# A transformer stack on one core: one product of the second feed-forward by 12-bit parts, and other engines for the last rows

## The chip, the cores and the metric

The kernel runs on one core of a Trainium2 chip. The time is device time in microseconds (us); a difference is judged between runs of the two kernels on the same chip. The core's engines are TensorE (PE, with its weight loads PEld), VectorE (DVE), ScalarE (ACT), GpSimd (POOL) and SyncE (SP), which here issues transfers. All times below are microseconds. L284 means line 284 of the kernel.

## The reference

Eight blocks are added one after the other to x, which has 2 x 256 tokens of 256 numbers, all in fp32: four times a cross-attention and a feed-forward, each behind a layer norm and a gate.

```python
x = x + tanh(g_xattn[0]) * _L0_xattn_ref(_layernorm(x), ctx_2048)
x = x + tanh(g_ffn[0])   * _L0_ffn_ref(_layernorm(x), ...)
x = x + tanh(g_xattn[1]) * _L1_xattn_ref(_layernorm(x), ctx_2048, ...)
x = x + tanh(g_ffn[1])   * _L1_ffn_ref(_layernorm(x), w_gate_up, w_down)
...
x = x + tanh(g_ffn[3])   * _L3_ffn_ref(_layernorm(x), ...)
```

Two of them are touched. The second feed-forward, with 1024 hidden columns:

```python
gate_up = jnp.einsum('bsh,oh->bso', h_shard, w_gate_up)
gate, up = jnp.split(gate_up, 2, axis=-1)
h = jax.nn.silu(gate) * up
out = jnp.einsum('bsi,hi->bsh', h, w_down)
```

And the last one, a mixture of 8 experts with the two best for each token (`_moe_routed`) beside a shared MLP of 704 hidden columns: each token gets the rows that its two experts made, times their weights, and the shared result. What matters of it is the end, `y.at[tok].add(w * gathered)`, `routed + shared`, and the gated addition to x.

## The kernel before

The 512 tokens are four tiles of 128 (n = 0 to 3); x stays in SBUF as four tiles of 128x256. The whole program is one function, `flamingo`. A scheduler places the instructions on each engine, except where the text fixes the order: `inline` (L222) chains an instruction behind the one before it in the list `line` (VectorE and what else is given to it), `pool_line` (GpSimd) or `pe_line` (TensorE).

**Two ways of multiplying in fp32.** A whole product (`chain`, L282) of 128x512 is two fp32 matmuls. A product by parts first cuts each operand into its top 12 bits and the rest, as fp32r: `weight_parts` (L625) cuts on VectorE (L596), copies the top on ScalarE (L631), subtracts on GpSimd (L632) to get the rest, and forms the difference of top and scaled rest on VectorE (L633). This last instruction can be held back and issued later (`held`). `three` (L640) then issues four matmuls of one sum ("same", L644) and two of another ("cross", L646), in two PSUM tiles, and `joined` (L648) joins them: ScalarE scales the cross sum out of PSUM (L649), VectorE adds the same sum (L650).

**The second feed-forward** (from L1108) runs over 8 chunks of 128 hidden columns. `whole1` makes a whole product, `parts1` one by parts, `silu1` is ScalarE's silu, `gated1` VectorE's product into hT (L1137). Chunks 0 to 2 are whole; of chunk 3 the gate is by parts and the up product whole; chunks 4 to 7 are by parts, with the PSUM pools taken in turn (ps_mm with 4 buffers, ps_acc with 2, ps_tr with 2). The parts of the gate's columns (gate_parts) are made earlier, beside the attention; the parts of the up columns of chunks 4 and 5, then 6 and 7 (up_parts) are made here by `columns_parts`, in two pieces of 128x512. Then `down` multiplies hT with the down weights for each of the four token tiles. On SP follow the loads for the next block, and on GpSimd the zeroing of the arrays that later take scattered rows (L1202 to L1205).

**The end.** The experts' rows lie in DRAM (yg). For each token tile n, L2029 loads its two rows (k = 0 and 1) into rows[n], tiles 0 and 2 on SP's queue, 1 and 3 on ScalarE's. The shared MLP's sum of a tile is made by `shared_down` on TensorE; `add_to_x` (L286) adds scaled rows or sums to x on VectorE (L287). `final(n)` (L2033) adds a tile's two rows: for tile 2, row 1 goes over ScalarE (scaling, L2037) and GpSimd (addition, L2038). Tile 3's two rows are added by TensorE instead, as two more matmuls of its sum, with diagonal matrices that hold the weights (`spread`, made by GpSimd, L1916). `store(n)` (L2042) writes a tile on SP's queue.

The lines of chunks 2 and 3, and the order of the end:

```python
    gated1(2, silu1(pa), pb)
    diffs.pop()()
    g = parts1(3, gate_parts, 3, ps_tr, "tr")
    pb = mm()
    whole1(3, up1, pb)
    columns_parts(up_parts, ffn1[1], 4, 6, 2, diffs)
    gated1(3, silu1(g), pb)
    diffs.pop()()
```

Of the kernel before, what the change touches and what calls it, by code (L numbers as in the profile page):

```python
# [17 lines left out]
F32 = mybir.dt.float32  # L18
F32R = mybir.dt.float32r
I32 = mybir.dt.int32  # L20
U8 = mybir.dt.uint8
AF = mybir.ActivationFunctionType
ALU = mybir.AluOpType
AX = mybir.AxisListType

P = 128
NT = 4
D = 256
# [22 lines left out]
def flamingo(ctx: ExitStack, tc: tile.TileContext, a: dict, out: bass.AP):  # L51
    nc = tc.nc

    def pool(name, bufs, space=None):
        kw = {} if space is None else {"space": space}
        return ctx.enter_context(tc.tile_pool(name=name, bufs=bufs, **kw))

    const = pool("const", 1)
    q4 = pool("q4", Q4)
    q2 = pool("q2", Q2)  # L60
    q1 = pool("q1", 4)
# [4 lines left out]
    x = const.tile([P, NT, D], F32, name="x")  # L66
# [73 lines left out]
    ident = const.tile([P, P], F32, name="ident")  # L140
# [49 lines left out]
    def gf(layer):  # L190
        return tg[:, 4 + layer : 5 + layer]
# [30 lines left out]
    def inline(i, line=line):  # L222
        if line:
            if line[-1] is not None:
                behind(i, line[-1], "in the order of the text")
            line[:] = [i]
        return i
# [35 lines left out]
    def batch(t, k, ts=slice(0, T)):  # L263
        return t[:, ts.start // 256 : ts.stop // 256, k, :]
# [14 lines left out]
    def mm(shape=None):  # L279
        return ps_mm.tile(shape or [P, 512], F32, tag="mm", name="mm")  # L280

    def chain(dst, pairs):  # L282
        for i, (lhsT, rhs) in enumerate(pairs):
            inline(nc.tensor.matmul(dst, lhsT=lhsT, rhs=rhs, start=(i == 0), stop=(i == len(pairs) - 1)), pe_line)  # L284

    def add_to_x(n, acc, scalar, cols=slice(0, D)):  # L286
        return inline(nc.vector.scalar_tensor_tensor(x[:, n, cols], acc, scalar, x[:, n, cols], ALU.mult, ALU.add))  # L287
# [231 lines left out]
    for s in range(18):  # L519
        n = s // 4  # L520
# [53 lines left out]
    ps_mm = pool("ps_mm", 4, bass.MemoryType.PSUM)  # L574
# [51 lines left out]
    def weight_parts(dst, src, t, last=None, held=None):  # L626

        i = inline(cut(t, src))
        if last is not None:
            behind(i, last, "in turn, where there is room")  # L630
        nc.scalar.copy(dst[0], t)  # L631
        nc.gpsimd.tensor_sub(dst[1], src, t)  # L632
        diff = lambda: inline(nc.vector.scalar_tensor_tensor(dst[2], dst[1].bitcast(F32), -1.0 / EPS, t, ALU.mult, ALU.add))  # L633
        if held is None:
            diff()
        else:
            held.append(diff)
        return i

    def three(same, cross, left, right):  # L640

        for k in range(2):
            for i in range(2):
                inline(nc.tensor.matmul(same, lhsT=left(i, k), rhs=right(i, k), start=(k == 0 and i == 0), stop=(k == 1 and i == 1)), pe_line)  # L644
        for k in range(2):
            inline(nc.tensor.matmul(cross, lhsT=left(2, k), rhs=right(2, k), start=(k == 0), stop=(k == 1)), pe_line)  # L646

    def joined(dst, same, cross, scale=1.0):  # L648
        nc.scalar.mul(dst, cross, -EPS * scale)  # L649
        return inline(nc.vector.scalar_tensor_tensor(dst, same, (1.0 + EPS) * scale, dst, ALU.mult, ALU.add))  # L650
# [197 lines left out]
    def l1_scales(sums, part):  # L848

        r, g = (small.tile(list(sums.shape), F32, tag=f"{nm}{sums.shape[2]}", name=nm, bufs=2) for nm in ("rsum", "gsum"))  # L850
        inline(nc.vector.reciprocal(r, sums))
        inline(nc.vector.tensor_scalar_mul(g, r, gx(1)))
        for t, v in ((all_t, sums), (all_r, r)):
            nc.gpsimd.tensor_add(t[:, 0:part], t[:, 0:part], v.rearrange("p i j -> p (i j)"))
        return g

    def l1_turned(d, groups=4):
        tr = ps_acc.tile([P, 2, P], F32, tag="acc", name="tr1")
        rows = 32 * groups
        for i in range(2):  # L860
            inline(nc.tensor.transpose(tr[:, i, 0:rows], d[0:rows, i * P : (i + 1) * P], ident[0:rows, 0:rows]), pe_line)
        sums = small.tile([P, 2, groups], F32, tag=f"sum{groups}", name="sum1", bufs=2)
        nc.scalar.copy(sums, tr[:, :, 0:rows:32])
        return l1_scales(sums, 2 * groups)
# [15 lines left out]
    ffn1 = []  # L880
# [45 lines left out]
    def columns_parts(w, src, base, c, chunks, held=None):  # L926

        t = q2.tile([P, 2, chunks * P], F32, tag="q2", name="c_top")
        cols = slice((c - base) * P, (c - base + chunks) * P)
        weight_parts([w[:, j, :, cols] for j in range(3)],  # L930
                     src.rearrange("p (k e) -> p k e", k=2)[:, :, c * P : (c + chunks) * P], t, held=held)
# [10 lines left out]
    for h in range(16):  # L942
        g, hl = h // 4, h % 4
# [8 lines left out]
        for b in range(B):  # L952
# [12 lines left out]
            if h and h % 2 == 0:  # L965
                if b == 0:
                    sums1 = l1_sums([totals.pop((h - 2 + i, c)) for i in range(2) for c in range(B)])
                else:
                    scale = l1_turned(sums1)
# [23 lines left out]
            if hl and g < 3:  # L993
                n = 2 * (hl - 1) + b
# [9 lines left out]
    scale = l1_turned(sums1, 3)  # L1004
# [4 lines left out]
    t = totals.pop((15, 1))  # L1009
# [15 lines left out]
    scale = l1_scales(sums, 2)  # L1025
# [25 lines left out]
    def negatives(z):  # L1051
        t = q2.tile(list(z.shape), F32, tag="q2", name="fm")
        inline(nc.vector.tensor_scalar_min(t, z, 0.0))
        nc.scalar.activation(t, t, AF.Exp)
        return t
# [60 lines left out]
    gate1, up1 = (w.rearrange("p (k e) -> p k e", k=2) for w in ffn1[0:2])  # L1116
# [3 lines left out]
    def whole1(c, w, p, ts=slice(0, T)):  # L1120
        chain(p[:, ts], [(w[:, k, c * P : (c + 1) * P], batch(xT, k, ts)) for k in range(2)])

    def parts1(c, w, base, pool, tag):
        same, cross = (pool.tile([P, T], F32, tag=tag, name="gu1") for _ in range(2))
        cols = slice((c - base) * P, (c - base + 1) * P)
        three(same, cross, lambda i, k: w[:, i, k, cols], lambda i, k: batch(x_parts[i], k))
        t = q2.tile([P, T], F32, tag="q2", name="gu1")
        joined(t, same, cross)
        return t

    def silu1(src):
        s = q2.tile([P, T], F32, tag="q2", name="silu")
        silus[:] = [nc.scalar.activation(s, src, AF.Silu)]
        return s

    def gated1(c, s, up):
        inline(nc.vector.tensor_mul(hT[c // 2][:, c % 2, :], s, up))  # L1137
# [12 lines left out]
    for c in range(2):  # L1150
        for w, p in zip((gate1, up1), ps[c]):
            whole1(c, w, p, lasts)
        s = silu1(ps[c][0])
# [3 lines left out]
    pa, pb = mm(), mm()  # L1157
    whole1(2, gate1, pa)
    whole1(2, up1, pb)
    diffs = []  # L1160
    columns_parts(up_parts, ffn1[1], 4, 4, 2, diffs)
    gated1(2, silu1(pa), pb)
    diffs.pop()()
    g = parts1(3, gate_parts, 3, ps_tr, "tr")
    pb = mm()
    whole1(3, up1, pb)
    columns_parts(up_parts, ffn1[1], 4, 6, 2, diffs)
    gated1(3, silu1(g), pb)
    diffs.pop()()
    pools = deque([(ps_mm, "mm"), (ps_acc, "acc"), (ps_tr, "tr")])  # L1170
    for c in range(4, 8):
        g, u = [], []
        for w, base, to in ((gate_parts, 3, g), (up_parts, 4, u)):
            to.append(parts1(c, w, base, *pools[0]))
            pools.rotate(-1)
            if to is g:
                s = silu1(g[0])
# [130 lines left out]
    t = negatives(early)  # L1308
# [193 lines left out]
    t, u = rtile(), place  # L1502
# [45 lines left out]
    t = rtile()  # L1548
# [13 lines left out]
    row = q2.tile([P, T], F32, tag="q2", name="row")  # L1562
# [241 lines left out]
    es, t = l3_exps(0, ps3[0])  # L1804
    g = l3_sums(0, t)
    es1, t1 = l3_exps(1, ps3[1])
    load_table(AF.Silu, exps[-1], "the feed-forward's table")
    for b in range(B):
        if b:
            es, g = es1, l3_sums(1, t1)  # L1810
# [101 lines left out]
    kept = const.tile([P, 2, NT], F32, name="kept")  # L1912
    nc.vector.tensor_scalar(w[:, 0, :], w[:, 1, :], -0.5, 0.5, ALU.mult, ALU.add)
    nc.vector.tensor_scalar(w[:, 1, :], w[:, 1, :], 0.5, 0.5, ALU.mult, ALU.add)
    nc.vector.scalar_tensor_tensor(kept, slot3, float(E * CAP), w, ALU.is_lt, ALU.mult)
    spread = q1.tile([P, 2, P], F32, tag="q1", name="spread")  # L1916
    for k in range(2):
        nc.gpsimd.tensor_scalar(spread[:, k, :], ident, kept[:, k, 3:4], None, ALU.mult)
    nc.vector.tensor_scalar_mul(kept, kept, gf(3))

    def shared_down(n, more=[]):
        acc = ps_acc.tile([P, D], F32, tag="acc", name="acc")
        chain(acc, [(hS[c // 2][:, c % 2, n * P : (n + 1) * P], shd[:, c, :]) for c in range(6)] + more)
        return acc
# [5 lines left out]
    for g in range(5):  # L1930
        t = q4.tile([P, 2, D + 1], F32, tag="q4", name="xg_sb")
# [93 lines left out]
    accs = [shared_down(n) for n in range(2)]  # L2025
    rows = []
# [3 lines left out]
        after_all(read, returned)  # L2030
        rows.append(o)

    def final(n):  # L2033
        for k in (1, 0):
            if (n, k) == (2, 1):
                t = q1.tile([P, D], F32, tag="q1", name="row2")
                nc.scalar.activation(t, rows[n][:, k, :], AF.Copy, scale=kept[:, k, n : n + 1])  # L2037
                nc.gpsimd.tensor_add(x[:, n, :], x[:, n, :], t)  # L2038
                continue
            add_to_x(n, rows[n][:, k, :], kept[:, k, n : n + 1])  # L2040

    def store(n):  # L2042
        nc.sync.dma_start(out[n * P : (n + 1) * P, :], x[:, n, :])

    for n in range(2):
        add_to_x(n, accs[n], gf(3))
    accs = [shared_down(2), shared_down(3, [(spread[:, k, :], rows[3][:, k, :]) for k in range(2)])]
    add_to_x(2, accs[0], gf(3))
    final(0)
    store(0)  # L2050
    for n in (1, 2):
        final(n)
        store(n)
    add_to_x(3, accs[1], gf(3))
    store(3)
    line.clear()
# [656 lines left out]
```

## Time and profile before

| what | us |
|---|---|
| median of 3 runs (545.74 to 546.36) | 546.23 |
| the profiled execution, whole | 545.36 |
| its span | 543.5 |
| TensorE busy | 535.0 |
| VectorE busy | 332.3 |
| ScalarE busy | 238.1 |
| GpSimd busy | 124.7 |

The span is that of one execution under the profiler, on the one core, from the first instruction to the end of the last; the mean granted TensorE clock in it was 0.998 of full speed. What the execution took beyond the span (1.86) lies before and after it. TensorE's busy time hides what it does: the page's groups separate whole products (L284) and those by parts (L644, L646).

The page's rows of the 40 slices, each of 13.6 us, show where TensorE is not full: the first and the last slice, and no other.

```
PE   8999999999999999999999999999999999999996
PEclk9999999999999999999999999999999999999999
DMA  8910120000004000040000404599030799614013
```

The second feed-forward lies in the slices from about 340 to 380, the end of the kernel in the last one. In a row of the profile's timeline, the first number is the start in the span, the second the duration, then engine, line, operation, the tiles that are written and read, and the shapes; in brackets stands how long the engine was idle before and what it waited for.

### The profile page before, as it was taken

The numbers are of one execution on the slowest core, as the hardware profiler recorded it, in microseconds if no ns is written. First come the engines' busy times: TensorE is split into PE (matmuls) and PEld (weight loads), VectorE is DVE, ScalarE is ACT, GpSimd is POOL, SyncE is SP. The second block draws the span as 40 slices with busy tenths as digits, with TensorE's granted clock in tenths as the row PEclk, the third lists the DMA queues.
The fourth block names the chain that finished last, engine by engine and source line by source line (L and its number), as shares of the span: only waits on it lengthen the run. The fifth ranks groups of instructions, "written<-read, shape, count | busy, mean of one in ns | idle before, by whom it ended". The sixth has DMA issues, their size and how long they took to land.

```text
span 543.5 us, 8726 instructions
## 1 busy us (share of the span) xinstructions
PE 535.0 (98%) x3304; PEld 395.4 (73%) x3304; DVE 332.3 (61%) x777; ACT 238.1 (44%) x488; POOL 124.7 (23%) x229
## 2 busy tenths in 40 slices
PE   8999999999999999999999999999999999999996
PEld 6554775878888888887888888687776447884465
DVE  6999797745556454754547567765467536562322
ACT  6886466644354434444444533451433212422320
POOL 5776104111031110311012223112022001252150
PEclk9999999999999999999999999999999999999999
DMA  8910120000004000040000404599030799614013
GB/s 289 427 45 0 30 125 1 1 1 0 1 0 153 2 2 1 1 154 1 0 1 1 156 1 156 232 300 390 27 143 13 279 411 244 246 40 129 19 46 132
DMA packets 15528, 57.06 MB, mean 105 GB/s; under 512 B 2653, under 2 KB 5924, under 8 KB 12102
## 3 DMA queue, kind: packets, MB, share of 16 engines
q1 hardware_dynamic: 13718, 51.61, 25.9%
q0 software_dynamic: 1472, 4.28, 2.3%
q8 instruction: 28, 0.46, 0.3%
q10 hardware_dynamic: 288, 0.52, 0.3%
q14 instruction: 22, 0.18, 0.1%
HBM read 51.60 MB, written 5.25 MB: 105 GB/s over the span
## 4 chain that ended last, share of the span: by engine, by line
PE 94%; DVE 3%; ACT 1%; issue 0%; POOL 0%
PE mm L284 27%; PE acc L284 20%; PE mm L644 9%; PE mm L646 4%; PE mm L1590 4%; PE s L464 3%; PE acc L476 2%; PE q L644 2%; PE mm L1951 2%; PE acc L1616 2%; PE gu L644 2%; PE outT L721 1%; PE acc L1973 1%; PE q L646 1%; PE mm L1414 1%; PE y L1647 1%
## 5 line engine op out<-in xcount | busy, mean ns | idle before, releaser
L284 PE MATMUL mm<-qT,kT 128*128 128x256 f32 x256 | 60.7, 381 | 0.0
L284 PE MATMUL acc<-e,v 128*128 128x256 f32 x256 | 60.6, 379 | 0.0
L284 PEld LDWEIGHTS mm<-qT,kT 128*128 128x128 f32 x256 | 48.1, 190 | 9.2 <-ACT oT L836 1.6
L284 PEld LDWEIGHTS acc<-e,v 128*128 128x128 f32 x256 | 48.3, 189 | 8.2 <-issue 0.4
L632 POOL TENSOR_TENSOR h_parts<-w,h_top 128x256 fp32r<-128x256 f32 x28 | 20.8, 742 | 139.2 <-PE acc L284 73.6
L825 ACT ACTIVATE e<-mm 128x512 f32<-128x512 f32 x64 | 38.1, 598 | 22.3 <-PE mm L284 22.1
L828 DVE TENSOR_TENSOR t<-e,e 128x512 f32<-128x512 f32 x32 | 22.1, 691 | 23.6 <-ACT e L825 23.4
L468 ACT ACTIVATE e<-s 128x512 f32<-128x512 f32 x64 | 32.9, 605 | 5.5 <-PE s L464 5.4
L236 POOL TENSOR_TENSOR rstd<-mv,eps_ln 128x1 f32<-128x1 f32 x31 | 6.7, 217 | 108.8 <-DVE mv L235 108.8
L649 ACT ACTIVATE v<-mm 128x512 f32<-128x512 f32 x24 | 14.3, 597 | 31.1 <-PE mm L646 31.1
L644 PE MATMUL mm<-ctx_top,h_parts 128*128 128x512 f32 x56 | 27.3, 488 | 0.0
L284 PE MATMUL acc<-w,oT 128*128 128x256 f32 x112 | 26.8, 381 | 0.1
L836 ACT COPY oT<-acc 128x256 f32<-128x256 f32 x32 | 11.9, 372 | 34.2 <-PE acc L284 34.2
L650 DVE SCALAR_TENSOR_TENSOR v<-mm,v 128x512 f32<-128x512 f32 x24 | 16.6, 692 | 16.6 <-ACT v L649 16.6
L649 ACT ACTIVATE kT<-mm 128x512 f32<-128x512 f32 x28 | 16.7, 598 | 20.5 <-PE mm L646 20.5
L287 DVE SCALAR_TENSOR_TENSOR x<-acc,gsum,x 128x256 f32<-128x256 f32 x56 | 23.6, 477 | 2.8 <-PE acc L284 2.2
L650 DVE SCALAR_TENSOR_TENSOR kT<-mm,kT 128x512 f32<-128x512 f32 x28 | 19.3, 689 | 6.7 <-ACT kT L649 6.7
L284 PEld LDWEIGHTS acc<-w,oT 128*128 128x128 f32 x112 | 20.1, 190 | 3.5 <-ACT oT L836 0.5
L644 PE MATMUL mm<-v_parts,ctx_top 128*128 128x512 f32 x48 | 22.1, 461 | 0.0
L644 PE MATMUL mm<-ctx_rest,h_parts 128*128 128x512 f32 x56 | 22.0, 393 | 0.0
L464 PE MATMUL s<-w_q,ctx_nat 32*128 32x256 f32 x256 | 21.1, 400 | 0.2 <-ACT e L468 0.2
L650 DVE SCALAR_TENSOR_TENSOR qT<-q,qT 128x512 f32<-128x512 f32 x14 | 9.7, 692 | 18.4 <-ACT qT L649 18.4
(444 smaller groups left out, 1182.0 us busy)
## 6 DMA issues: line engine op xcount, KB each, us to landing
gu<-in_l_gu_all SPq DMA_DIRECT2D x14, 1024.0 KB, 7.6
w<-in_l_all SPq DMA_DIRECT2D x4, 2048.0 KB, 8.6
dn<-in_l_dn_all SPq DMA_DIRECT2D x4, 1024.0 KB, 6.2
dn<-in_l_dn_all SPq DMA_DIRECT2D x6, 512.0 KB, 9.3
gu<-in_l_gu SPq DMA_DIRECT2D x4, 704.0 KB, 18.6
ctxT<-in_ctxT SPq DMA_DIRECT2D x4, 512.0 KB, 10.9
ctx_nat<-in_ctx SPq DMA_DIRECT2D x3, 512.0 KB, 7.2
dn<-in_l_dn SPq DMA_DIRECT2D x2, 704.0 KB
```

The costliest lines, as they stand in the source:

```text
L284: inline(nc.tensor.matmul(dst, lhsT=lhsT, rhs=rhs, start=(i == 0), stop=(i == len(pairs) - 1)), pe_line)
L287: return inline(nc.vector.scalar_tensor_tensor(x[:, n, cols], acc, scalar, x[:, n, cols], ALU.mult, ALU.add))
L464: in_turn(nc.tensor.matmul(ps[j][:, k, :], lhsT=ctx_nat[rows, b, hf, c * P : (c + 1) * P], rhs=qm[rows, n, i, :], start=True, stop=True))
L468: exps.append(nc.scalar.activation(es[j], ps[j], AF.Exp))
L632: nc.gpsimd.tensor_sub(dst[1], src, t)
L644: inline(nc.tensor.matmul(same, lhsT=left(i, k), rhs=right(i, k), start=(k == 0 and i == 0), stop=(k == 1 and i == 1)), pe_line)
L646: inline(nc.tensor.matmul(cross, lhsT=left(2, k), rhs=right(2, k), start=(k == 0), stop=(k == 1)), pe_line)
L649: nc.scalar.mul(dst, cross, -EPS * scale)
L650: return inline(nc.vector.scalar_tensor_tensor(dst, same, (1.0 + EPS) * scale, dst, ALU.mult, ALU.add))
L825: nc.scalar.activation(e, s, AF.Exp)
L828: nc.vector.tensor_add(t, es[0], es[1])
L1590: inline(nc.tensor.matmul(ps[j * BLK : (j + 1) * BLK, :], lhsT=xsT[k][:, block * BLK : (block + 1) * BLK], rhs=gu2[home(q, j)][:, at : at ...
```

## The change

There are two independent edits.

The first is in the second feed-forward: chunk 3's up product is made by parts instead of whole. A new tile, up3_parts, takes the parts of these 128 columns; `columns_parts` is called for it (a 128x256 piece, its difference not held back) ahead of the one for chunks 4 and 5, and `parts1` replaces `whole1`. It uses two buffers of ps_mm where the whole product used one. The silu of chunk 3 is now written ahead of that product.

The second is at the end: TensorE adds only row 0 of tile 3, so `spread` is one diagonal matrix instead of two; row 1 of tile 3 is added by VectorE. Tiles 1 and 2 each have their row 1 scaled by ScalarE and added by GpSimd (`final_aside`), where before only tile 2 had. The order of the additions is written out anew.

```diff
@@ second feed-forward
     whole1(2, up1, pb)
     diffs = []
+    up3_parts = q4.tile([P, 3, 2, P], F32R, tag="q4", name="up3_parts")
+    columns_parts(up3_parts, ffn1[1], 3, 3, 1)
     columns_parts(up_parts, ffn1[1], 4, 4, 2, diffs)
     gated1(2, silu1(pa), pb)
     diffs.pop()()
     g = parts1(3, gate_parts, 3, ps_tr, "tr")
-    pb = mm()
-    whole1(3, up1, pb)
+    s = silu1(g)
+    u = parts1(3, up3_parts, 3, ps_mm, "mm")
     columns_parts(up_parts, ffn1[1], 4, 6, 2, diffs)
-    gated1(3, silu1(g), pb)
+    gated1(3, s, u)
     diffs.pop()()
@@ the weights of the last rows
-    spread = q1.tile([P, 2, P], F32, tag="q1", name="spread")
-    for k in range(2):
-        nc.gpsimd.tensor_scalar(spread[:, k, :], ident, kept[:, k, 3:4], None, ALU.mult)
+    spread = q1.tile([P, P], F32, tag="q1", name="spread")
+    nc.gpsimd.tensor_scalar(spread, ident, kept[:, 0, 3:4], None, ALU.mult)
@@ the end
-    def final(n):
-        for k in (1, 0):
-            if (n, k) == (2, 1):
-                t = q1.tile([P, D], F32, tag="q1", name="row2")
-                nc.scalar.activation(t, rows[n][:, k, :], AF.Copy, scale=kept[:, k, n : n + 1])
-                nc.gpsimd.tensor_add(x[:, n, :], x[:, n, :], t)
-                continue
-            add_to_x(n, rows[n][:, k, :], kept[:, k, n : n + 1])
+    def final(n, k):
+        add_to_x(n, rows[n][:, k, :], kept[:, k, n : n + 1])
+
+    def final_aside(n):
+        t = q1.tile([P, D], F32, tag="q1", name="row")
+        nc.scalar.activation(t, rows[n][:, 1, :], AF.Copy, scale=kept[:, 1, n : n + 1])
+        nc.gpsimd.tensor_add(x[:, n, :], x[:, n, :], t)
...
-    accs = [shared_down(2), shared_down(3, [(spread[:, k, :], rows[3][:, k, :]) for k in range(2)])]
+    accs = [shared_down(2), shared_down(3, [(spread, rows[3][:, 0, :])])]
     add_to_x(2, accs[0], gf(3))
-    final(0)
+    for k in range(2):
+        final(0, k)
     store(0)
-    for n in (1, 2):
-        final(n)
-        store(n)
+    final_aside(1)
+    final(2, 0)
+    final_aside(2)
+    final(1, 0)
+    store(1)
+    store(2)
+    final(3, 1)
     add_to_x(3, accs[1], gf(3))
     store(3)
```

In the built program SP's queue takes the stores in the order of tiles 0, 2, 1, 3.

## Prediction, before the changed kernel was run

> **What bounds the kernel now.** I read the page's span and busy shares first, then the shares of the chain that ended last, then that chain in order of time at the two edited places.
>
> ```profile
> span 543.5 us, 8726 instructions
> ...
> PE 535.0 (98%) x3304; PEld 395.4 (73%) x3304; DVE 332.3 (61%) x777; ACT 238.1 (44%) x488; POOL 124.7 (23%) x229
> ...
> PE 94%; DVE 3%; ACT 1%; issue 0%; POOL 0%
> ```
>
> TensorE is busy for 98% of the span and makes 94% of the chain. So matmul time removed anywhere is time gained, unless TensorE then waits, and a wait put on TensorE is time lost. In order of time, the chain around the edited chunk reads (start, duration, what):
>
> ```profile
> 348.98 0.93 PE gu L644 x4
> 349.91 0.46 PE gu L646 x2
> 350.36 1.72 PE mm L284 x4
> ...
> 357.56 0.91 PE gu L644 x4
> ...
> 381.30 5.44 PE mm L284 x20
> ```
>
> The reader is to see that the same 128x512 product, gate of chunk 3 and up of chunk 3, costs 0.93 + 0.46 = 1.39 in parts and 1.72 whole, and that TensorE goes from one to the other with no gap. The line at 357.56 is the gate of chunk 6, which will matter.
>
> **Part A, the up product of chunk 3: what TensorE saves.** 1.72 - 1.39 = 0.33 (0.35 with the 0.91 + 0.46 of later chunks). If nothing else changed, A were -0.34.
>
> **Part A: what it adds to the other engines.** The same preparation exists for one 128x256 piece of weights (gate, chunk 7, at 322), so each added piece has a row: DVE cut 0.28, ACT cast 0.41, POOL subtraction 0.84, DVE difference 0.43. After the product come one ACT scaling (L649, 0.58) and one DVE join (L650, 0.69). These are small beside the idle time of DVE (39% of the span) but they are put in order into a place where a chain DVE to POOL to DVE to ACT is already running. Timeline rows (start, duration, engine, line, what, in brackets the idle time before and its releaser):
>
> ```profile
> 322.47 0.84 POOL L632 TENSOR_TENSOR gate_parts<-ffn,c_top 128x256 fp32r<-128x256 f32 x1 [3.16 <-DVE c_top L596]
> 323.34 0.43 DVE L633 SCALAR_TENSOR_TENSOR gate_parts<-gate_parts,c_top 128x256 fp32r<-128x256 f32 x1 [0.62 <-POOL gate_parts L632]
> ...
> 352.14 1.29 POOL L632 TENSOR_TENSOR up_parts<-ffn,c_top 128x512 fp32r<-128x512 f32 x1 [2.92 <-DVE c_top L596]
> 352.42 0.69 DVE L1137 TENSOR_TENSOR hT<-silu,mm 128x512 f32<-128x512 f32 x1 [0.36 <-ACT silu L1133]
> 353.46 0.69 DVE L633 SCALAR_TENSOR_TENSOR up_parts<-up_parts,c_top 128x512 fp32r<-128x512 f32 x1 [0.35 <-POOL v L1223]
> 354.13 0.69 DVE L650 SCALAR_TENSOR_TENSOR gu<-gu,gu 128x512 f32<-128x512 f32 x1
> 355.40 0.58 ACT L649 ACTIVATE gu<-gu 128x512 f32<-128x512 f32 x1
> ```
>
> DVE takes its instructions in order. The difference for chunks 6 and 7 (353.46) starts when POOL's subtraction ends (352.14 + 1.29 = 353.43), and behind it stands the join of gate 4 (354.13); silu of chunk 4 waits for that join, and the scaling of up 4 (355.40, ends 355.98) stands behind the silu on ACT. That scaling frees an accumulator that gate 6 writes, at 357.56. Its slack is 1.58 now, and 1.58 - 0.35 = 1.23 once TensorE is earlier.
>
> Now I walk the new order with these durations, 0.04 to 0.09 for each handover and an overlap of about 0.08 between neighbours on DVE. Cut of chunk 3 at 347.38 to 347.67 (its cast on ACT lies beside), POOL's subtraction 347.75 to 348.6, difference 348.63 to 349.06. Only then the cut for chunks 4 and 5, 348.98 to 349.40 (before: 347.38). POOL 349.48 to 350.76, difference 350.79 to 351.48. Join of gate 3 at 351.40 to 352.09 (before 351.03), silu to 352.76, scaling of up 3 to 353.25, its join 353.28 to 353.97. The cut for chunks 6 and 7 stands behind that join: 353.89 to 354.31 (before 351.64). POOL 354.39 to 355.68, difference 355.71 to 356.40, join of gate 4 at 356.32 to 357.01: 2.19 later than before. silu 4 to 357.68, scaling of up 4 at 357.59 to 358.17. TensorE comes to gate 6 at 357.56 - 0.35 = 357.21 and may start at about 358.22: a stall of 1.0, that is 0.66 later than before. The inputs of the products between (parts of chunks 4 and 5) are ready in time: the difference that ends at 351.48 is needed by up 4 at about 354.
>
> After a stall TensorE's first products are slower: the 20 records from 381.30, which follow a wait, take 5.44; by the pace of full rows, 16 of 256 columns at 0.215 (1.73 for eight) and four of 512 at 0.43 (1.72 for four) make 5.16, so about 0.25 more. A = 0.66 + 0.25 = **+0.9**. Then the gates and ups 6 and 7, the 64 down matmuls and the products from 381.30 follow one another with TensorE as the bound, so the shift reaches the end. Bounds: -0.34 if the wait does not form; +1.3 if chunk 7 also comes late for the down product (I put its last product at 369.15, against about 369.3 where it is needed). Also moved: SP's load of the next weights and POOL's two zeroing transfers, which wait for POOL's second subtraction and DVE's third product, so they start 2.2 later; the context load queued behind them on SP lands late by as much or less in a stretch where the DMA share is 1.0. I put it at the time of its need: 0 to 0.3 more, taken as 0.
>
> **Part B, the last rows.** Timeline rows of the end:
>
> ```profile
> 535.20 1.91 DVE L287 SCALAR_TENSOR_TENSOR x<-o3g,kept,x 128x256 f32<-128x256 f32 x4
> 536.32 0.51 ACT L2037 ACTIVATE row<-o3g,kept 128x256 f32<-128x256 f32 x1 [9.09 <-DMA o3g<-yg]
> 536.91 0.78 POOL L2038 TENSOR_TENSOR x<-x,row 128x256 f32<-128x256 f32 x1 [7.14 <-ACT row L2037]
> 537.73 0.48 DVE L287 SCALAR_TENSOR_TENSOR x<-o3g,kept,x 128x256 f32<-128x256 f32 x1 [0.62 <-POOL x L2038]
> 538.25 0.48 DVE L287 SCALAR_TENSOR_TENSOR x<-acc,tg,x 128x256 f32<-128x256 f32 x1
> ...
> 538.76 1.13 SPq L2043 DMA_DIRECT2D out_x<-x  x1
> ```
>
> TensorE ends at 538.23, the last addition follows at 538.25, the last store at 538.76. One matmul of two halves leaves: 0.43, so TensorE ends at 537.80. DVE keeps six additions after that of tile 2; ACT and POOL get one operation each more. Without contention: tile 1's second row arrives by 536.15 (DVE reads it then); I take 535.75. ACT 535.8 to 536.3, POOL 536.37 to 537.15, second POOL addition to 537.9; DVE 536.3 to 536.8 (tile 2), 537.2 to 537.67 (tile 1), 538.15 (tile 3), 538.6 (last). SP stores in the order of tiles 0, 2, 1, 3, each issue 0.47 after the other at least (the two row loads on SP stand at 531.51 and 531.99): tile 2 at 537.95, tile 1 at 538.4, tile 3 at 538.9. B = +0.1, and not the -0.43 that TensorE alone would give: DVE's row of additions is late next.
>
> **The rule against it.** POOL and DVE have already met with two inputs from SBUF each:
>
> ```profile
> 157.16 0.74 POOL L632 TENSOR_TENSOR h_parts<-w,h_top 128x256 fp32r<-128x256 f32 x1
> ...
> 157.24 1.22 DVE L633 SCALAR_TENSOR_TENSOR v_parts<-v_parts,w_top 128x512 fp32r<-128x512 f32 x1 [1.35 <-POOL v_parts L632]
> ```
>
> The same difference takes 0.69 at 353.46; here it takes 1.22, and ends 0.56 after POOL ends (157.90): it stood still for 0.53. The Trainium skill, page "SBUF — State Buffer", section "Who interferes with whom", says so: a VectorE instruction with two SBUF inputs and a GpSimd instruction that reads SBUF exclude each other for a whole instruction. The row at 352.42, with one input from PSUM, kept its 0.69 beside POOL's 1.29, as the page has it too. The five additions of rows in the tail read o3g and x, both in SBUF. The two POOL additions cannot lie beside them. By the lock: DVE to 536.16; tile 2's addition 536.3 to 536.8, POOL 536.7 to 537.4, then POOL's second and DVE's two left in turn, 0.74 + 2 x 0.48 = 1.70, to about 539.05, and the addition of the accumulator to 539.5. Last store at 539.55, against 538.76: B = **+0.8**. I take the lock, as its nearest row shows it; the +0.1 stays as an end. Above: with the second POOL addition last, tile 2's store starts at 539.3 and two more follow it on SP: +1.3. Below: the last store's issue took 1.13 where the other three take 0.34; were that short, 0.8 less.
>
> **Sum.** 0.9 + 0.75 = +1.65. The profiled execution took 545.36 (its span 543.5 and 1.86 around it), so 547.0 by its own time; it lies 0.87 under the median of 546.23, and on the median the forecast is **547.9**.
>
> **Rivals.**
> 1. *Stall, but the tail level* (+0.9 + 0.1 = +1.0, 547.2). For it: POOL has only one addition that surely meets DVE. Against it: the row at 157.24.
> 2. *The products come early after all*, on the other side: the scaling of up 4 is done before gate 6. This decides once DVE's chain is less than 1.2 late instead of 2.2, as when the difference of chunks 6 and 7 were put after the join of gate 4. Then A = -0.34, and with no lock and a short last issue B = -0.8: -1.1, 545.1. With the lock it is -0.34 + 0.75 = +0.4, 546.6.
> 3. *More is late*: the context load lands late (+0.3), chunk 7 late (+0.4), stores in a queue (+0.5): +2.6, 548.8.
>
> **How the numbers follow.** A difference under 0.2%, 1.1 us, is what a measurement here cannot tell from none. Chances: forecast (both) 0.45; stall alone 0.17; early products with the lock 0.13; early products without it 0.14; more late 0.11. Slower by over 0.2%: most of the first (0.42), half of the second (0.08), all of the last: 0.60. Faster: the better part of the early case without lock, 0.11. The rest, 0.29, is the same. The range runs from 545.2, the early case, to 549.0.
>
> **What would show it.** A right: the first matmul of gate 6 at about 358.2 after a stall of 1.0 released by ACT's L649, the join of gate 4 at about 356.3 behind a difference that waited for POOL. Wrong: gate 6 at 357.2. B right: a DVE addition or a POOL addition in the tail of 1.0 or more instead of 0.48 or 0.78, and the last store issued about 0.8 later relative to TensorE's end plus 0.43. Wrong: all keep their durations and TensorE's end sets the last addition.

## The result, and the profile after

The changed kernel takes 548.39 (median of 6 runs, 547.82 to 548.86) against 546.18 for the kernel before on the same chip: 1.0039 times as long, 95% interval 1.0026 to 1.0052. That is 2.1 more, with 1.4 to 2.8 as its interval. Its profiled execution took 548.16, with a span of 546.4.

The page of the changed kernel, the lines that answer to those of before (span, busy time, chain by engine):

```profile
span 546.4 us, 8737 instructions
...
PE 534.7 (98%) x3304; PEld 395.1 (72%) x3304; DVE 333.9 (61%) x780; ACT 239.4 (44%) x491; POOL 126.2 (23%) x230
...
PE 90%; DVE 5%; POOL 1%; ACT 1%; issue 1%; DMA 1%; DVEq 0%; POOLq 0%; SPq 0%
```

TensorE did lose work: 535.0 of busy time became 534.7. (Its number of records is the same, because a product by parts has six where a whole one has four, and the matmul left out at the end had two.) But its share of the chain fell from 94% to 90%, and VectorE's rose from 3% to 5%. The busy shares hardly moved; the chain did. Where it moved stands in the chain of waits of the changed kernel around the edited chunk (start, duration, what; pieces under 0.1 and a stretch marked with dots are left out):

```profile
342.08 5.30 PE mm L284 x20
347.38 0.53 issue
347.91 0.73 POOL up_parts L632
...
353.38 0.69 DVE gu L650
354.06 0.35 DVE c_top L596
354.48 1.67 POOL up_parts L632
356.18 0.69 DVE up_parts L633
356.88 0.61 DVE gu L650
357.56 0.49 issue
358.05 0.59 ACT gu L649
358.68 1.20 PE gu L644 x4
```

For eleven microseconds the chain holds no TensorE piece at all: it goes through the row that the prediction walked, cut, subtraction, difference, join, scaling, and comes back to TensorE at gate 6 (358.68). The line with 1.67 is the one that the prediction had at 1.29. Gate 6's first four products take 1.20 where the others take 0.91. Most of this 0.29 is a matter of counting: in a full row the chain counts a product from the end of the one before it, while the records overlap. By the single records, the second product of gate 6 starts 0.34 after the first, and 0.23 after it in a full row, so the restart itself costs 0.11.

**Comparing stages.** Executions differ at their start, mostly by some tenths, so I measure from an instruction ahead of the change, the last of VectorE's subtractions on line 922 (344.99 in the first profile of before, 345.09 in the changed kernel). As the end of the stage I take the start of a key product of the next block, which follows the first sixteen records of products behind the norms. TensorE's timeline before, and in the changed kernel:

```profile
384.86 1.88 PE L284 MATMUL mm<-ffn_l,ctxT 128*128 128x512 f32 x4
```

```profile
386.36 1.88 PE L284 MATMUL mm<-ffn_l,ctxT 128*128 128x512 f32 x4
```

The key product starts 39.87 after the mark before and 41.27 after it in the changed kernel: the first edit costs 1.40 by the end of its stage. (The chain would give 1.56, because it counts the sixteen products from the end of the transposes where those are late, at 382.96, and from their own start where they are not.) The loads of the experts' rows, 150 later, are a second mark for the end of the kernel.

**A difference that is not the change's.** The first profile of before has its row loads at 186.52 from the mark, the changed kernel at 188.61, which is 0.7 more than the stage lost. A second profile of the kernel before (below) explains it. One of VectorE's last copies ahead of the loads, in the first profile of before and in its second one:

```profile
524.27 0.42 DVE L204 COPY o<-acc 128x256 f32<-128x256 f32 x1 [0.83 <-PE acc L1973]
```

```profile
525.10 0.42 DVE L204 COPY o<-acc 128x256 f32<-128x256 f32 x1 [1.57 <-PE acc L1973]
```

From the mark, this copy is 0.7 late in the second, though TensorE's products that it waits for are not; in the changed kernel (526.43) it is as late, once the 1.40 of the stage is taken off. GpSimd's next scatter of an expert's rows waits for this copy (idle for 1.36 in the second profile), the others follow at their usual pace, and the row loads come 0.7 later. ScalarE's last copy there is 1.6 late in the same executions, with no releaser on an engine, but the scatters keep their pace past it. It happens with the old end and with the new one, in nine of the fourteen profiles. So the fair partner of the changed kernel's profile is the second one of before: span 544.5, row loads at 187.22, and a loss of 1.39 at the loads, the same as at the end of the stage. In these two profiles the chain goes through the row loads at the end (3.7 from issue to landing); in before's first profile it is TensorE that the last addition waits for.

**The end.** VectorE's row additions that were slowed, GpSimd's two, and SP's last three stores, in the timeline of the changed kernel (three views, one for each engine):

```profile
538.03 0.84 DVE L287 SCALAR_TENSOR_TENSOR x<-o3g,kept,x 128x256 f32<-128x256 f32 x1
...
539.58 0.94 DVE L287 SCALAR_TENSOR_TENSOR x<-o3g,kept,x 128x256 f32<-128x256 f32 x1
```

```profile
537.86 0.73 POOL L2040 TENSOR_TENSOR x<-x,row 128x256 f32<-128x256 f32 x1 [5.89 <-ACT row L2039]
539.41 0.83 POOL L2040 TENSOR_TENSOR x<-x,row 128x256 f32<-128x256 f32 x1 [0.82 <-ACT row L2039]
```

```profile
540.27 0.34 SPq L2043 DMA_DIRECT2D out_x<-x  x1
540.70 1.46 SPq L2043 DMA_DIRECT2D out_x<-x  x1
542.24 0.38 SPq L2043 DMA_DIRECT2D out_x<-x  x1
```

The two additions beside GpSimd's take 0.84 and 0.94 instead of 0.48, as the lock says. Yet the last addition starts 6.92 after the row loads, against 6.86 in before's second profile: it is not later. The last store is. It starts 8.54 after the row loads, against 7.39 before. The store of tile 2, second on SP, waits for GpSimd's second addition (539.41 + 0.83 = 540.24), and the other two stand behind it. But the start of a store is not yet the end of the kernel. One issue among the last two is long, 1.46 of the third store here and 1.09 of the last one in before's second profile, so the last issue ends at 8.92 after the row loads against 8.48, and the span ends 12.7 after them against 12.2.

### The profile page after: what moved, and what is told of

Read it like the earlier page. It is cut to its first block, busy times and chain, and to the rows that moved or that the text cites. A ratio compares the mean times of both kernels' runs of the same rounds, so it can differ in the third digit from the quotient of the medians.

```text
span 546.4 us, 8737 instructions
## 1 busy us (share of the span) xinstructions
PE 534.7 (98%) x3304; PEld 395.1 (72%) x3304; DVE 333.9 (61%) x780; ACT 239.4 (44%) x491; POOL 126.2 (23%) x230
## 4 chain that ended last, share of the span: by engine, by line
PE 90%; DVE 5%; POOL 1%; ACT 1%; issue 1%; DMA 1%; DVEq 0%; POOLq 0%; SPq 0%
PE mm L284 26%; PE acc L284 18%; PE mm L644 9%; PE mm L646 4%; PE mm L1592 4%; PE s L464 3%; PE acc L476 2%; PE q L644 2%; PE mm L1952 2%; PE acc L1618 2%; PE outT L721 1%; PE acc L1974 1%; PE q L646 1%; PE mm L1416 1%; PE y L1649 1%; DVE x L287 1%
```

## The experiments

Ratios are to the kernel before on the same chip, with 95% intervals. "Stage" is the start of the key product from the mark; "last store" is the start of the last store's issue from the row loads, and its end.

| run | ratio | stage | last store |
|---|---|---|---|
| before (two profiles) | | 39.87, 39.87 | 7.25 to 8.38, 7.39 to 8.48 |
| the changed kernel | 1.0039 (1.0026 to 1.0052) | 41.27 | 8.54 to 8.92 |
| a_only | 1.0032 (1.0021 to 1.0044) | 41.31 | 7.28 to 8.66 |
| a_ht3_later | 1.0025 (1.0016 to 1.0035) | 40.85 | 7.50 to 8.64 |
| a_cut67_first | 1.0006 (0.9997 to 1.0015) | 40.32 | 7.33 to 8.58 |
| a_reordered | 1.0003 (0.9994 to 1.0011) | 39.97 | 7.27 to 8.61 |
| a_reord_norm | 1.0002 (0.9992 to 1.0012) | 39.92 | 7.25 to 8.38 |
| after_norm | 1.0036 (1.0022 to 1.0049) | 41.21 | 8.71 to 9.47 |
| after_reordered | 1.0018 (1.0009 to 1.0026) | 39.98 | 7.30 to 8.46 |
| b_only (two profiles) | 1.0009 (1.0000 to 1.0018) | 39.86, 39.88 | 8.18 to 8.56, 8.04 to 8.70 |
| b_all_dve | 1.0008 (0.9999 to 1.0017) | 39.88 | 7.56 to 7.89 |
| b_no_aside1 | 1.0005 (0.9994 to 1.0017) | 39.87 | 7.73 to 8.35 |

A time is known to about 0.1%, 0.5; the stage column repeats within 0.02 between kernels that agree in the second feed-forward (b_only, b_all_dve, b_no_aside1, before), and carries the finer readings.

**Each edit alone.** a_only is the first edit with the end as before; b_only the second with the feed-forward as before.

> The first edit alone (chunk 3's up product by parts; the end as before). Theory (the delayed chain on VectorE and GpSimd stalls TensorE ahead of gate 6): slower than before by 1.3 to 1.6, TensorE's gate 6 about 1.1 later than before, POOL's subtraction for chunks 6 and 7 at 1.67 instead of 1.29. Rival (the loss is all in the tail, and the products of the second feed-forward come early): faster by about 0.3.

> The second edit alone (the last rows; the second feed-forward as before). Theory of the lock: slower than before by 0.6 to 0.9, with at least two of VectorE's row additions at 0.8 or more instead of 0.48. Rival (TensorE's end sets the last addition): faster by about 0.4. Third (no lock, VectorE's row is level): +0.1. If the row loads are late by 0.7 as in the changed kernel, that comes from this edit, and adds to it.

The first edit alone has the whole loss of its stage, 41.31 - 39.87 = 1.44, and 0.32% in time: the rival is out. The second alone costs 0.09%, 0.5 (0.0 to 1.0). Only one of VectorE's additions in it was stretched to 0.84 instead of two, and its row loads, late by 0.7 in this profile, were late in before's second profile as well, so they are not its doing.

**The subtraction of 1.67.** a_ht3_later moves the product of chunk 3 behind the join of gate 4:

```diff
-    u = parts1(3, up3_parts, 3, ps_mm, "mm")
+    u3 = parts1(3, up3_parts, 3, ps_mm, "mm")
...
-    gated1(3, s, u)
+    s3 = s
     diffs.pop()()
...
             if to is g:
                 s = silu1(g[0])
+                if c == 4:
+                    gated1(3, s3, u3)
```

> The first edit alone, with VectorE's product of chunk 3 (two inputs from SBUF) moved behind the join of gate 4, so that it no longer lies beside POOL's subtraction. Theory of the lock: the subtraction falls from 1.67 to 1.29, gate 6 comes about 0.38 earlier than in the first edit alone, and the time is 0.3 to 0.4 shorter than that. Rival (the subtraction is long for another reason, such as transfers): it stays at 1.6 to 1.7, and nothing is gained.

In the changed kernel VectorE's product of chunk 3 and GpSimd's subtraction lie side by side (two views of it), and then the subtraction of a_ht3_later:

```profile
354.31 0.68 DVE L1137 TENSOR_TENSOR hT<-silu,gu 128x512 f32<-128x512 f32 x1
```

```profile
354.48 1.67 POOL L632 TENSOR_TENSOR up_parts<-ffn,c_top 128x512 fp32r<-128x512 f32 x1 [3.61 <-DVE c_top L596]
```

```profile
355.07 1.29 POOL L632 TENSOR_TENSOR up_parts<-ffn,c_top 128x512 fp32r<-128x512 f32 x1 [3.61 <-DVE c_top L596]
```

Before, the product read silu from SBUF and the up product from PSUM (`hT<-silu,mm`). By parts the up product is joined in SBUF, so the same instruction now has two SBUF inputs. That this is the difference, and not that VectorE was first, shows chunk 2 in the changed kernel, whose up product is still whole: there VectorE's product also starts ahead of a subtraction of GpSimd, and that one keeps its 1.29 (two views):

```profile
349.34 0.68 DVE L1137 TENSOR_TENSOR hT<-silu,mm 128x512 f32<-128x512 f32 x1
```

```profile
349.58 1.29 POOL L632 TENSOR_TENSOR up_parts<-ffn,c_top 128x512 fp32r<-128x512 f32 x1 [0.94 <-DVE c_top L596]
```

With chunk 3's product out of the way its subtraction is back at 1.29 as well, gate 6 starts 0.4 earlier than in a_only and the stage is 41.31 - 40.85 = 0.46 earlier. The lock is shown at this place. The time moved in the same direction, by less than its interval.

**The order on VectorE.** a_cut67_first issues the cut for chunks 6 and 7 ahead of the join of up 3; a_reordered adds the move of the product.

```diff
     g = parts1(3, gate_parts, 3, ps_tr, "tr")
+    columns_parts(up_parts, ffn1[1], 4, 6, 2, diffs)
     s = silu1(g)
     u = parts1(3, up3_parts, 3, ps_mm, "mm")
-    columns_parts(up_parts, ffn1[1], 4, 6, 2, diffs)
```

> The first edit alone, with the cut for chunks 6 and 7 issued on VectorE ahead of the join of up 3 instead of behind it. Theory (TensorE's stall ahead of gate 6 comes from the order of the chain on VectorE): the subtraction for chunks 6 and 7 starts about 1.9 earlier, the join of gate 4 about 1.0 earlier than in the first edit alone, gate 6's stall shrinks from about 1.3 to 0.3, and the time falls by about 1.0, to before's +0.2 to +0.5. Rival (the stall is due to the mere number of operations added to VectorE, ScalarE and GpSimd): the time stays within 0.4 of the first edit alone.

> Both moves at once on the first edit alone: the cut for chunks 6 and 7 ahead of the join of up 3, and the product of chunk 3 behind the join of gate 4. Theory: the scaling of up 4 ends before TensorE comes to gate 6, so no stall; TensorE keeps the 0.34 of the products by parts; time 0 to 0.4 shorter than before and about 1.5 shorter than the first edit alone. Rival (number of operations): within 0.4 of the first edit alone.

One line moved, and 0.99 of the stage's 1.44 is gone, with 0.26% of the time; every operation that the edit added is still there. So the stall comes from the order, not from the number of operations. With both moves gate 6 no longer waits: it starts 0.32 earlier than before. But the stage is at 39.97, still 0.10 later than before, where I had expected to see TensorE's 0.34 as a gain.

**What was left.** In a_reordered the scheduler has put VectorE's norm of tile 0 and a key product behind the addition of tile 2's down sum, and before it had them ahead. VectorE's timeline in a_reordered, and in a_reord_norm, which issues the down product of tile 2 only behind them (`down` for tile 2 and for tile 3 called from the loop over the norms, after tile 0 and after tile 2):

```profile
375.08 0.42 DVE L234 BATCH_NORM_STATS2 st<-x 128x6 f32<-128x256 f32 x1
```

```profile
374.16 0.42 DVE L234 BATCH_NORM_STATS2 st<-x 128x6 f32<-128x256 f32 x1
```

The statistics of tile 1 start at 375.08 in the one and at 374.16 in the other: 0.92, at the head of a row of norms (statistics, GpSimd's root, scaling, tile after tile) that ends just ahead of the products. How much of it TensorE feels is another matter.

> The first edit alone with both moves, and VectorE's norm of tile 0 (and the key product after it) again ahead of the addition of tile 2's down sum, as it stands before the change; in the first edit the scheduler had put it behind. Theory (this order is why the reordered first edit gave nothing: bn of tile 1 starts 0.9 later and the row of norms up to tile 3 ends last): the products after the norms start about 0.6 earlier than in the reordered first edit, and the time is 0.2 to 0.4 under before. Rival (the products by parts save nothing at the end for another reason, such as the context load): same start as in the reordered first edit, time as before.

> The changed kernel with that order of the norms alone restored (the stall ahead of gate 6 left in). Theory: TensorE is late by about 1.3 anyway, so the order is worth 0.2 to 0.3 here: products after the norms 1.3 later than before instead of 1.55, time about 2.0 over before. Rival (the order of the norms, not the stall, is the main loss): the time falls by 0.9 or more.

In a_reord_norm the stage comes to 39.92: 0.05 earlier instead of 0.6, and still 0.05 after before. So the expectation of a gain was wrong, and the order of the norms was not what took it. TensorE's weight loads say who does (PEld, in a_reord_norm, then in before's second profile):

```profile
362.42 0.30 PEld L646 LDWEIGHTS gu<-up_parts 128*128 128x128 f32 x2 [0.35 <-DVE gu L650]
...
368.27 1.59 PEld L284 LDWEIGHTS mm<-ffn_l,hT 128*128 128x128 f32 x8 [0.35 <-DVE hT L1137]
```

```profile
362.29 0.41 PEld L646 LDWEIGHTS gu<-up_parts 128*128 128x128 f32 x2
...
367.21 2.46 PEld L284 LDWEIGHTS mm<-ffn_l,hT 128*128 128x128 f32 x12 [0.16 <-DVE hT L1137]
```

TensorE comes to the last chunks 0.34 early and waits longer for VectorE's joins and for the last product. VectorE has one join of 0.69 more to do ahead of them: from the mark, its joins of gates 4 to 7 come 0.85 to 0.87 later than before. By the last down product TensorE is 0.05 behind before. after_norm puts the order of the norms back in the changed kernel: 41.27 - 41.21 = 0.06 of the stage, less than the 0.2 to 0.3 expected (the 1.55 named there is the chain's figure for the 1.40 above), and the stall remains the main loss.

> The changed kernel with both moves in the second feed-forward, its end left as it is. Theory: it loses the stall of the first edit and keeps the cost of the second, so it stands 0.2 to 0.7 over before and about 1.5 under the changed kernel. Rival: as the changed kernel, 2.2 over before.

With the feed-forward reordered and the changed end, the time falls from 0.39% to 0.18% over before. The remainder, against a_reordered's 0.03%, is again the second edit's: 0.84 between the means of these two runs, which were made on the same chip (0.4 to 1.2, by their scatter).

**The end.** b_all_dve lets VectorE add all seven rows; b_no_aside1 keeps GpSimd's addition for tile 2 alone, and TensorE's one matmul is still moved. Their orders after the addition of tile 2's shared sum:

```diff
-    final_aside(1)
-    final(2, 0)
-    final_aside(2)
+    final(1, 1)
     final(1, 0)
     store(1)
+    final(2, 1)      # b_no_aside1: final_aside(2)
+    final(2, 0)
     store(2)
     final(3, 1)
```

> The second edit alone, with nothing given to ScalarE and GpSimd: VectorE adds all seven rows, two more than in the second edit. Theory of the lock: seven additions in a row take 3.3, less than five of VectorE and two of GpSimd that exclude each other (3.9), so it is about 0.4 shorter than the second edit, and 0.2 to 0.4 longer than before. Rival (no lock): two more additions on VectorE make it 0.2 to 0.9 longer than the second edit.

> The second edit alone without the new ScalarE and GpSimd row of tile 1: VectorE adds both rows of tile 1, tile 2 is as before, and one matmul of TensorE is still given to VectorE. Theory (what TensorE gives up was not on the path, and VectorE's row is late next): 0.3 to 0.5 over before, no better than the second edit. Rival (the new GpSimd addition is the whole cost of the second edit): at or below before.

By time the three ends cannot be told apart (1.0009, 1.0008, 1.0005, each within 0.1%), so b_all_dve decides nothing about the price of the lock there. None of them is under before.

> The kernel before, unchanged, profiled a second time. The profiles of the changed kernel and of four variants all have ScalarE's last copy ahead of the shared sums 1.6 late (2.9 idle, released by nothing on an engine) and the row loads 0.7 late; the first profile of before has neither. Theory (it is a matter of the execution, not of the change): a second profile of before can have it too, with a span of about 544.3. Rival (the change brings it): the second profile is as the first, span 543.5.

> The second edit alone, profiled a second time: its first profile took 546.28 where the median of its runs is 547.36, so it does not show what the slower executions do. Theory (GpSimd's and VectorE's additions exclude each other more or less, by the order in which the rows land): the five additions of rows on VectorE take about 3.0 instead of 2.55, and the last addition starts about 6.9 after the row loads instead of 6.45. Rival (the difference lies in the stores): the last addition stands as in the first profile, and the stores end later.

before_again gave the late copies and the span of 544.5 that were told above. In b_only_again the copies are on time, and the last addition starts 6.28 after the loads, 0.46 earlier than in the first profile of before (6.74): what TensorE gave up does arrive there. My theory for this run was wrong, and the rival right in so far as the additions are not late. The last store's issue starts and ends about where it did in b_only's first profile, but its transfer lands 3.2 after that start instead of 1.9. Nor does the profile show what makes this edit slow: of the 2.5 by which its span is longer than b_only's first, 2.0 lie ahead of the mark, before either edit.

Four of five profiles with the changed end have the last store start at 8.0 to 8.7 after the loads, the seven with the old end at 7.25 to 7.50; after_reordered is the exception (7.30). One issue among the last two takes 0.7 to 1.6, and falls on the last store with the old end and mostly on the one before with the new, so most of this shift is only its place. By the end of the last issue the two groups overlap, 8.4 to 8.7 with the old end and 8.5 to 9.5 with the new, and so they do by the end of the span, 12.0 to 12.7 after the loads and 12.0 to 13.2. So the second edit costs something by the time of its runs (b_only, after_reordered), and is no gain, but which step of the end it loses it in stays open.

## Why the prediction was right or wrong

The direction was right, and so was the mechanism of the first edit; the sum of 1.65 was short of 2.1. That it came so near is in part luck: the first edit was put 0.5 too low, the second, at 0.75 against a measured 0.5 (0.0 to 1.0), perhaps too high, and by a way that the runs do not show. By its steps:

- **The chain that stalls gate 6**: right. The join of gate 4 started at 356.79 (put at 356.32) behind a difference that waited for GpSimd, and ScalarE's scaling of up 4 released gate 6 at 358.68 (put at 358.22). a_cut67_first and a_reordered show that the order made it.
- **The durations in the walk**: one was mis-sized, and it is most of what A lacks. GpSimd's second subtraction was taken at 1.29 and took 1.67. The prediction used the lock against the tail, and cited the product `hT<-silu,mm` as the row that escapes it, but did not see that the edit itself turns this product's second input from PSUM into SBUF. a_ht3_later takes 0.4 off the start of gate 6 by moving it.
- **The first products after a stall**, taken 0.25 slower: right as a sum, not as a cause. The restart is 0.11. The rest lies in the time from which the prediction counted: 357.56 is the end of the product before gate 6, whose own record starts at 357.40. By starts, gate 6 is 1.17 late and its second product 1.28, where the prediction has 0.66 + 0.25 = 0.91.
- **The shift reaches the end with TensorE as the bound**: nearly. The 1.28 is 1.30 at the last down product and 1.40 at the end of the stage, where TensorE waits for the norms; the scheduler's other order of them is worth 0.06 there (after_norm). The loss is still 1.39 at the row loads.
- **-0.34 if the wait does not form**, the other side's rival: its condition was met in a_reord_norm, and the gain did not come. VectorE's longer row takes the 0.34 back.
- **The tail at +0.75 by the lock**: the size stands within the measured 0.5 (0.0 to 1.0), the way to it is not shown. The stretched additions are there (0.84 and 0.94, not the 1.0 named), but the last addition is not later, since before's own row waits 0.6 to 0.75 for GpSimd as well. The last store does start 1.15 later in the changed kernel than in before's second profile, as the prediction's upper end has it, but its issue ends only 0.44 later.
- **The loads that start later**, taken as 0: nothing in the chain of the changed kernel waits for them.
- **Small sums**: the terms listed under the third rival add up to +2.85, not +2.6, and the two row loads on SP stand 0.44 apart, not 0.47. Neither touches the forecast.

## What to carry to other kernels

When one engine is 98% busy, work taken off it is a gain only if the engines that feed it in that stage have room: here TensorE goes through a chunk by parts in 2.72, while the joins of gates 5, 6 and 7 on VectorE come 3.2 apart, before (357.35, 360.55, 363.76) as in a_reord_norm. Neither VectorE nor ScalarE is busy for 3.2; each waits more than 1 of it for the other: join of the gate, silu, scaling of the up product, its join, the product into hT, and only then the join of the next gate. Such a loop does not show in the busy shares. Before adding an operation to an engine that works in order, write down what stands behind it and who waits for that; moving one cut ahead of one join was worth 1.0 here. And when an edit changes where an operand lies, PSUM or SBUF, ask again which instructions now exclude each other.

## What was not expected of the hardware

GpSimd's subtraction was stretched by 0.38 by a VectorE product of 0.68 that had started 0.17 earlier, and a VectorE addition by 0.36 and 0.46 by GpSimd's additions of 0.73 and 0.83 that had started 0.17 earlier: in all three the one that started second was held, once GpSimd and twice VectorE, and by 0.1 to 0.2 less than a wait up to the recorded end of the first. In nine of fourteen profiles, of kernels with the old end and with the new, a copy of VectorE ahead of the row loads came 0.7 late without its input being late, and moved the loads by 0.7, and a copy of ScalarE came 1.6 late with no releaser on any engine; what holds them is not known.
